# A fused attention and mixture-of-experts layer on one core: norm rows moved to GpSimd, ScalarE's copies and the giving out of tiles placed anew, VectorE's relus ahead of ScalarE's

## The chip, the cores and the metric

The kernel runs on one core of a Trainium2 chip. The metric is the time of the whole kernel on the device, in microseconds. The core has five engines that the text calls by the names of the profile: PE (TensorE, the matmuls), DVE (VectorE), ACT (ScalarE), POOL (GpSimd) and SP (SyncE, which here only starts transfers). Each works through its own instructions in order; semaphores hold an instruction until what it reads is there, or until the buffer that it writes is free.

## The reference, cut to what matters

x is 8 sequences (batches in what follows) of 512 tokens of 128 features, float32. A layer of attention with 16 heads of 8 features, causal, then a layer of 8 experts, of which each token takes the best two:

```python
def _layernorm(x, axis=-1, eps=1e-05):
    m = jnp.mean(x, axis=axis, keepdims=True)
    v = jnp.var(x, axis=axis, keepdims=True)
    return (x - m) / jnp.sqrt(v + eps)
...
    q = (x @ Wq).reshape(b, t, H, HD); k = ...; v = ...
    s = jnp.einsum('bqhd,bkhd->bhqk', q * scale, k)
    s = jnp.where(causal[None, None], s, -jnp.inf)
    p = jax.nn.softmax(s, axis=-1)
    o = jnp.einsum('bhqk,bkhd->bqhd', p, v).reshape(b, t, H * HD)
    return o @ Wo + bo
...
    logits = x_flat @ gate_w.T
    probs = jax.nn.softmax(logits / TEMPERATURE, axis=-1)
    topk_probs, topk_idx = jax.lax.top_k(probs, TOPK)
    hidden = jax.nn.relu(jnp.einsum('th,ehf->tef', x_flat, w1) + b1[None])
    all_out = jnp.einsum('tef,efh->teh', hidden, w2) + b2[None]
    gathered = jnp.take_along_axis(all_out, topk_idx[:, :, None], axis=1)
    y_flat = jnp.sum(gathered * topk_probs[:, :, None], axis=1)
...
    x = x + attention(_layernorm(x), ...)
    x = x + experts(_layernorm(x), ...)
```

## The kernel before

**Attention** goes batch by batch, and in a batch by four groups g of four heads. For a group the scores are computed twice. `shifts` computes them with queries in rows (tiles "s", PE lines L623 and L628) only for the maximum of each row (tile "pm", DVE, L642); the maxima (nm, L648) are split into two bf16 parts by GpSimd (nh, L358), transposed by PE (nmTp, L588), copied by ScalarE (nmT, L590) and written by GpSimd's own DMAs (L596) as two more rows into the operand q of the second product. `attend` then computes the scores transposed (tiles "st", L783 and L788), already less the row's maximum; ScalarE's exp turns a bank of them into "pt" (L793), and PE multiplies pt with the values "va" into "po" (L704). At a group's end po is copied (ob), transposed (oqp, L725), divided (L728, L730), and at a batch's end transposed once more (oTp, L748; copy oT, L750) and projected (pp, L756; added to x on DVE, L760).

s and st share a ring of four PSUM banks (`ps_sc`): an s bank is freed by a row maximum on DVE, an st bank by an exp on ACT. Everything else goes through a ring of three banks (`ps_mm`).

**Ahead of a batch's attention** `norms` (for b = 0 and 1 `project` itself) runs `layernorm`: statistics of four blocks of 128 tokens on DVE (bn_stats, bn_aggr, L369 and L370), two small operations on GpSimd (ve, rstd, L358), and four rows xn on DVE (L384, 128x128 each). `project` transposes xn (xnTp on PE, copy xnT on ACT, L397), computes q and k, splits them into three bf16 parts each (ACT, DVE and a subtraction on GpSimd, L478), packs them through DRAM, adds the bias bo to x on GpSimd (L553), and computes the values (pv on PE, L567; copy va on ACT, L571).

**Experts.** When a batch's attention is done, `route` normalises it with the same `layernorm` (xn_f), computes the logits (pl, L834), picks two experts, counts, gives each token a slot and scatters its row into DRAM by GpSimd's indirect DMAs (L1052). After batches 1, 3, 5, 6 and 7 `dispatch` (steps s = 0 to 4, DVE L962 to L1024) gives out tiles of 128 slots, 8, 16, 16, 23 and 15 of them, while other batches still run. A tile of an expert is four matmuls with the first weights (ph, L1287), a relu of each of the four columns c of blocks into hT, and four with the second weights (py, L1146). The relus go c = 0, 1, 2, 3: ACT takes two of them (three, once attention is over), DVE the rest (L1294 and L1296). They write one tile hT, and its writes are kept in the order in which they were traced.

**What orders the work.** Each of these parts is a Python generator that yields the time at which it wants to go on, in units of one batch; a loop always advances the one with the smallest time. For PE, ACT, DVE and SP the order in which instructions are traced in this way is the order on the engine. GpSimd's go through `G_ops`, which keeps program order as well. So a number such as `b - 1.84` is a place in the queue, and no wait by itself. In `route`, `soon(n)` moves its clock on by n steps; a step is 0.018 of a batch for b = 1, 3 and 5 and 0.025 for 0, 2 and 4, 0.012 for 6 and 7. The expert tiles have planned times of their own (`TILES_AT`), the first at 3.3.

```python
    TILES_AT = ((3.3, 0.24), (5.35, 0.12), (7.5, 0.055), (8.4, 0.03), (9.1, 0.03))
...
        while lanes:
            lane = min(lanes)
            try:
                lane[0] = max(lane[0], next(lane[2]))
```

Of the kernel before, what the change touches and what calls it, by code (L numbers as in the profile page):

```python
# [9 lines left out]
F32 = mybir.dt.float32  # L10
# [3 lines left out]
ALU = mybir.AluOpType  # L14
# [4 lines left out]
P = 128  # L19
# [7 lines left out]
def preln_attn_moe(ctx: ExitStack, tc: tile.TileContext, x, wq, wk, wv, wo, bo,  # L27
# [35 lines left out]
    nc = tc.nc  # L63
    V = nc.vector
    B, T, D = x.shape
    E, _, F = w1.shape
    H, HD = 16, 8
    NT = T // P
    G, HG = 4, 4
    NP = H // 2  # L70
    FC = F // P
# [33 lines left out]
    for k, b in ((0, 1), (0, 3), (0, 5), (0, 6), (1, 7)):  # L105
        n = GROUPS[k].index(b) + 1
# [14 lines left out]
    small = ctx.enter_context(tc.tile_pool(name="small", bufs=2))  # L121
# [18 lines left out]
    def load_x(b):  # L140
        t = const.tile([P, NT, D], F32, tag=f"x{b}", name=f"x_{b}")
        nc.sync.dma_start(out=t, in_=x[b].rearrange("(c p) d -> p c d", p=P))
        return t

    xt = {0: load_x(0)}
# [43 lines left out]
    for s in range(2):  # L189
# [3 lines left out]
        f = const.tile([P, P], BF16, tag=f"feature{s}", name=f"feature_{s}")  # L193
# [76 lines left out]
    def mm_tile(name):  # L270
        return ps_mm.tile([P, T], F32, tag="mm", name=name)
# [14 lines left out]
    for k in range(2):  # L286
        n = E * ROOM[k] + SPARE * P
# [77 lines left out]
    def layernorm(src, name, t, each):  # L365
        stats = small.tile([P, NT, 6], F32, tag="stats", name=f"stats_{name}")
        mv = small.tile([P, NT, 2], F32, tag="mv", name=f"mv_{name}")
        for c in range(NT):
            nc.vector.bn_stats(stats[:, c, :], src[:, c, :])  # L369
            nc.vector.bn_aggr(mv[:, c, :], stats[:, c, :])  # L370
            yield t[0] + each * (c + 1)
        rstd = small.tile([P, NT], F32, tag="rstd", name=f"rstd_{name}")
        ve = small.tile([P, NT], F32, tag="ve", name=f"ve_{name}")
        first = name in ("a0", "a1")
        on_pool = nc.gpsimd if first else G_ops
        on_pool.tensor_tensor(ve, mv[:, :, 1], eps, ALU.add)
        on_pool.tensor_tensor(rstd, ve, mhalf, ALU.pow)
        yield t[1]
        xn = work.tile(
            [P, NT, D if name[0] == "a" else XROW], F32, tag=f"xn{name[0]}", name=f"xn_{name}",  # L380
            bufs=1 if name[0] == "a" else XB,
        )
        for c in range(NT):
            nc.vector.tensor_scalar(  # L384
                xn[:, c, :D], src[:, c, :], mv[:, c, 0:1], rstd[:, c : c + 1],
                ALU.subtract, ALU.mult,
            )
            if c < NT - 1:
                yield t[1] + each * (c + 1)
        return xn  # L390

    def rows_T(xn, name):
        pt = mm_tile(f"xnTp_{name}")
        for c in range(NT):
            nc.tensor.transpose(pt[:, ts(c, P)], xn[:, c, :D], ident)
        xnT = work.tile([P, T], F32, tag=f"xnT{name[0]}", name=f"xnT_{name}", bufs=1)
        nc.scalar.copy(xnT, pt)  # L397
        return xnT


    normal = {}

    def norms():
        for b in range(2, B):
            yield b - 2.16
            normal[b] = yield from layernorm(xt[b], f"a{b}", (b - 2.16, b - 2.0), 0.025)


    packed, shifted, attended, added = set(), set(), set(), set()
# [2 lines left out]
    def project():  # L412
# [17 lines left out]
        for b in range(B):  # L430
            early = EARLY if b > 1 else 0.0
            if b < 2:
                yield b - 1.70
                xn = yield from layernorm(
                    xt[b], f"a{b}", (b - 1.70, b - (1.32 if b == 1 else 1.50)), 0.025
                )
            else:
                xn = normal.pop(b)
            if 0 < b < B - 2:
                xt[b + 2] = load_x(b + 2)  # L440
            yield b - (1.84 if b > 1 else 1.21 if b == 1 else 1.41)
            xnT = rows_T(xn, f"a{b}")
            late = 0.19 if b == 1 else 0.0
            yield b - (1.40 if early else 1.36) - early + late
# [2 lines left out]
            n = G if b == 0 else 2  # L447
# [112 lines left out]
                pack(0, 1)  # L560
                pack(1, 1)
            packed.add(b)
            yield b - 0.85
            assert b < 2 or b - 2 in added
            pv = mm_tile(f"pv_{b}")
            for c in range(NT):
# [245 lines left out]
    def route():  # L812
        for b in range(B):
# [6 lines left out]
            def soon(steps=1.0, least=0.0, step=step, least_of=float(b < B - 1)):  # L820
                now[0] += max(steps * step, least * least_of)
                return now[0]

            yield now[0]
            t = [soon(0), soon(7), soon(4 if b == B - 1 else 6)]
            xn2[b] = yield from layernorm(
                xt[b], f"f{b}", t, step / 2 if b == B - 1 else step
            )
# [38 lines left out]
            for k in range(2):  # L867
# [9 lines left out]
                f = pick[:, b, k, :].rearrange("p (c e) -> p c e", e=E)  # L877
# [64 lines left out]
            lanes.append([now[0], 100 + b, scatter(k, b, now[0])])  # L942
            for s, (_, after, _, _) in enumerate(STEPS):
                if after == b:
                    yield from dispatch(s, soon)


    def dispatch(s, soon):
# [130 lines left out]
    def when(s, i):  # L1079
        t0, pace = TILES_AT[s]  # L1080
        return t0 + pace * i

    def experts():
# [13 lines left out]
        def quad(s, i):  # L1097
            first = i - i % 4
            return first, min(4, STEPS[s][2] - first)

        def after(s, i):
            return when(s, quad(s, i)[0]) >= B

        def ahead(s, i):
            if not after(s, i):
                return 3

            late = [a for a in tiles if after(*a)].index((s, i))
            return min(WTS - 3, WTS // 2 - 2 + late)

        def behind(s, i):
            return 2 if after(s, i) else 1
# [27 lines left out]
        def second(s, i, hT):  # L1140
            first, m = quad(s, i)
            if i == first:
                yo[s, first] = work.tile([P, 4, D], F32, tag="yo", name=f"yo_{s}_{i}")
            py = mm_tile(f"py_{s}_{i}")[:, :D]
            for c in range(FC):
                nc.tensor.matmul(  # L1146
                    py, lhsT=hT[:, c, :], rhs=w2_sb[:, bass.ds(at[s, i] + c * E * D, D)],
                    start=(c == 0), stop=(c == FC - 1),
                )
            V.tensor_tensor(  # L1150
                yo[s, first][:, i - first, :], py, wt[s, i][:, F + FC :], ALU.add
            )
# [28 lines left out]
        def store(s, i):  # L1181
            k, b, _, last = STEPS[s]
            first, m = quad(s, i)
            ins = nc.gpsimd.indirect_dma_start(  # L1184
                out=ys[k],
                out_offset=bass.IndirectOffsetOnAxis(
                    ap=to[s, first][:, i - first : i - first + 1], axis=0
                ),
                in_=yo[s, first][:, i - first, :], in_offset=None,
            )  # L1190
            in_order(ins)
            for other in sent[k]:
                tc.declare_no_dep(
                    ins.ins, other, reason="every slot has its own row, or one nobody reads"
                )
            sent[k].append(ins.ins)
            if last and i == STEPS[s][2] - 1:
                tiled[k] = sent[k]
# [77 lines left out]
        for n, (s, i) in enumerate(tiles):  # L1276
            first, m = quad(s, i)
            yield when(s, i + 1)
            if after(s, i):
                ph = ps_sc.tile([P, T], F32, tag="sc", name=f"ph_{s}_{i}")  # L1280
                hT = work.tile([P, 2, T], F32, tag="pt", name=f"hT_{s}_{i}", bufs=6)
                hT = hT[:, 0, :].rearrange("p (c t) -> p c t", c=FC)
            else:
                ph = mm_tile(f"ph_{s}_{i}")
                hT = work.tile([P, FC, P], F32, tag="hT", name=f"hT_{s}_{i}")
            for c in range(FC):
                nc.tensor.matmul(  # L1287
                    ph[:, ts(c, P)], lhsT=wt[s, i][:, ts(c, P)],
                    rhs=turned[s, first][:, ts(i - first, P)], start=True, stop=True,
                )  # L1290
            for c in range(FC):
                bias = wt[s, i][:, F + c : F + c + 1]
                if c < (FC - 1 if after(s, i) else FC // 2):
                    nc.scalar.activation(hT[:, c, :], ph[:, ts(c, P)], AF.Relu, bias=bias)  # L1294
                else:
                    nc.vector.tensor_scalar(  # L1296
                        hT[:, c, :], ph[:, ts(c, P)], bias, 0.0, ALU.add, ALU.max
                    )
            yield when(s, i + 1.4)
            ready = late[: max(0, len(late) + 1 - behind(s, i))]  # L1300
            del late[: len(ready)]
            for part in ready:
                second(*part)
            yield when(s, i + 1.7)
            for part in ready:
                store(*part[:2])
            late.append((s, i, hT))
            fetch_to(n + 1 + ahead(s, i))
# [115 lines left out]
```

## Time and profile before

| what | value |
|---|---|
| median of 3 runs | 583.0 us (582.61 to 583.82) |
| the profiled execution's own time | 580.48 us |
| its span, first to last instruction | 578.8 us, granted PE clock 0.966 |
| PE busy | 506.7 us (88%) |
| DVE busy | 410.5 us (71%), 1272 instructions recorded |
| ACT busy | 307.3 us (53%) |
| POOL busy | 242.4 us (42%), 380 instructions recorded |
| first st of batches 1 to 7 | 88.3, 132.4, 178.4, 229.4, 280.3, 335.2, 389.8 us |
| row maxima (pm, L642) | 320, 680 ns each |
| exps (pt, L793) | 320, 599 ns each |

How to read the views. A row of instructions has start, duration, engine, line, operation, output and inputs by the program's names, and a count where several stand together; "[0.74 <-ACT pt L793]" behind it says that the engine was idle for 0.74 us before and that ScalarE's instruction of line 793 ended that. The waits of an engine are given as "who waited <- for whom: us in total, times, longest". The table by stretches has, for each engine, its busy time and the number of its instructions, then PEclk, the TensorE clock that was granted as a share of the full one, the share of DMA time, and GB/s. A busy PE can still be slow: where PEclk is 0.5, its matmuls take twice as long.

### The profile page before, as it was taken

How to read it: one execution, taken by the hardware profiler on the slowest of the kernel's cores; microseconds unless marked ns; L12 is line 12 of the kernel's file. 1: busy time of each engine (PE TensorE's matmuls, PEld its weight loads, DVE VectorE, ACT ScalarE, POOL GpSimd, SP SyncE). 2: the span in 40 equal slices, each digit the busy share in tenths (PEclk: the TensorE clock that was granted, in tenths of full speed). 3: DMA queues.
4: the chain of work that ended last, by engine and by line, in shares of the span. 5: the costliest groups of instructions: out<-in, count | busy, mean ns of one | idle time of the engine just before them, and what ended most of it. 6: DMA issues, size and time to landing. Idle time of an engine off the chain costs nothing. (4 is left out here: it accounts for less than half of the span.)

```text
span 578.8 us, 14044 instructions
## 1 busy us (share of the span) xinstructions
PE 506.7 (88%) x4762; PEld 373.9 (65%) x4762; DVE 410.5 (71%) x1272; ACT 307.3 (53%) x673; POOL 242.4 (42%) x380
## 2 busy tenths in 40 slices
PE   8868999988987989999899999998898889789980
PEld 6644556556544565665567777766576878689980
DVE  4987787887888779778978678787653445233694
ACT  3645666755754665575556555554564434245530
POOL 4032212405716423661753356345435524644442
PEclk9888899999998999999999999999999979989995
DMA  3728667288299572535526573222333686758783
GB/s 82 190 66 202 150 157 184 59 206 191 73 193 188 145 193 55 133 80 130 158 65 169 116 193 94 66 66 76 102 107 117 199 269 190 208 165 263 239 303 104
DMA packets 68761, 86.06 MB, mean 149 GB/s; under 512 B 11540, under 2 KB 50748, under 8 KB 66652
## 3 DMA queue, kind: packets, MB, share of 16 engines
q1 hardware_dynamic: 61508, 74.87, 50.0%
q0 software_dynamic: 6592, 9.65, 5.2%
q8 instruction: 39, 0.64, 0.5%
q10 hardware_dynamic: 592, 0.66, 0.5%
q14 instruction: 30, 0.25, 0.1%
HBM read 61.34 MB, written 26.16 MB: 151 GB/s over the span
## 5 line engine op out<-in xcount | busy, mean ns | idle before, releaser
L793 ACT ACTIVATE pt<-st 128x512 f32<-128x512 f32 x320 | 178.4, 599 | 109.0 <-PE st L783 49.3
L642 DVE TENSOR_REDUCE pm<-s 128x1 f32<-128x512 f32 (+2 forms) x320 | 205.5, 680 | 27.0 <-PE s L628 23.3
L1184 POOL DMA_INDIRECT ys<-yo,to x78 | 76.5, 980 | 99.1 <-ACT pt L793 32.4
L623 PE MATMUL s<-k,q 72*128 72x384 bf16 (+2 forms) x384 | 93.3, 278 | 15.8 <-ACT pt L793 9.9
L628 PE MATMUL s<-k,q 128*128 128x128 bf16 x512 | 94.1, 223 | 7.9 <-ACT pt L793 5.2
L783 PE MATMUL st<-q,k 128*128 128x128 bf16 x512 | 91.0, 220 | 10.2 <-DVE pm L642 5.5
L704 PE MATMUL po<-pt,va 128*18 128x512 f32 (+3 forms) x1024 | 91.6, 444 | 1.4 <-ACT pt L793 1.4
L788 PE MATMUL st<-q,k 74*128 74x256 bf16 (+2 forms) x384 | 91.9, 276 | 0.0
L1146 PE MATMUL py<-w_sb,hT 128*128 x624 | 87.4, 283 | 4.5 <-DVE have L962 2.2
L1146 PEld LDWEIGHTS py<-w_sb,hT 128*128 128x128 f32 x624 | 78.8, 197 | 7.8 <-issue 5.2
L1052 POOL DMA_INDIRECT xs<-xn_f,slot x64 | 64.0, 1000 | 30.9 <-ACT pt L793 15.6
L628 PEld LDWEIGHTS <-q 128*128 128x128 bf16 x512 | 50.9, 100 | 32.2 <-issue 29.2
L623 PEld LDWEIGHTS <-q 72*128 72x128 bf16 x384 | 37.6, 99 | 39.8 <-issue 32.2
L783 PEld LDWEIGHTS <-k 128*128 128x128 bf16 x512 | 50.9, 100 | 4.0
L788 PEld LDWEIGHTS <-k 74*128 74x128 bf16 x384 | 37.4, 98 | 22.7 <-issue 17.2
L596 POOL DMA_DIRECT2D q<-nmT x64 | 34.1, 536 | 39.5 <-ACT nmT L590 37.2
L358 POOL CAST nh<-nm 128x16 bf16<-128x16 f32 x28 | 5.6, 198 | 91.8 <-DVE nm L648 90.8
L1296 DVE TENSOR_SCALAR hT<-ph,wt 128x128 f32<-128x128 f32 x72 | 21.9, 346 | 28.8 <-ACT hT L1294 23.5
L704 PEld LDWEIGHTS po<-pt,va 128*18 128x18 f32 x1024 | 22.7, 96 | 30.1 <-issue 21.8
L1294 ACT ACTIVATE hT<-ph,wt 128x128 f32<-128x128 f32 x72 | 22.6, 364 | 35.7 <-issue 12.3
L1287 PE MATMUL ph<-xgT,wt 128*128 128x128 f32 x288 | 40.1, 282 | 0.7 <-issue 0.4
L1287 PEld LDWEIGHTS ph<-xgT,wt 128*128 128x128 f32 x288 | 35.0, 191 | 5.6 <-issue 2.7
(185 smaller groups left out, 697.6 us busy)
## 6 DMA issues: line engine op xcount, KB each, us to landing
wt<-wrows SPq DMA_DIRECT2D x36, 322.0 KB
k<-kparts SPq DMA_DIRECT2D x42, 192.0 KB
q<-wrows SPq DMA_DIRECT2D x24, 322.0 KB
k<-wrows SPq DMA_DIRECT2D x18, 322.0 KB
q<-qparts SPq DMA_DIRECT2D x30, 192.0 KB
q<-ys SPq DMA_DIRECT2D x15, 256.0 KB
k<-xs SPq DMA_DIRECT2D x42, 65.0 KB
qparts<-part SPq DMA_DIRECT2D x14, 192.0 KB
```

Of the source, the lines that this page charges most:

```text
L596: ins = nc.gpsimd.dma_start(out=q2_buf[b % 2][KS + l : KS + l + 1, HG * g : HG * g + HG], in_=nmT[16 * l : 16 * l + 16],)
L623: nc.tensor.matmul(ps[:, at : at + t * P], lhsT=q2[:KS, h, q], rhs=k2[:KS, h, : t * P], start=(at == 0), stop=True, skip_group_check=True,)
L628: nc.tensor.matmul(ps[:, at + t * P : at + (t + 1) * P], lhsT=q2[:, h, q], rhs=k2[:, h, q], start=(at + t == 0), stop=True, skip_group_che ...
L642: nc.vector.tensor_reduce(top, src, AX.X, ALU.max)
L704: nc.tensor.matmul(po[32 * h : 32 * h + 2 * VC, j * P :], lhsT=va[:, j, c0 : c0 + 2 * VC], rhs=at_cols(pts[pr], unit, u, at, W), start=(fi ...
L783: nc.tensor.matmul(ps[:, at : at + P], lhsT=k2[:, h, k], rhs=q2[:, h, k], start=(at == 0), stop=True, skip_group_check=True,)
L788: nc.tensor.matmul(ps[:, at + P : at + T - j * P], lhsT=k2[:KO, h, k], rhs=q2[:KO, h, (j + 1) * P :], start=False, stop=True, skip_group_c ...
L793: last_exp[0] = nc.scalar.activation(pt[:, v, :], ps, AF.Exp, scale=SCALE)
L1052: ins = nc.gpsimd.indirect_dma_start(out=xs[k], out_offset=bass.IndirectOffsetOnAxis(ap=slot[b][:, j * NT + i : j * NT + i + 1], axis=0), ...
L1146: nc.tensor.matmul(py, lhsT=hT[:, c, :], rhs=w2_sb[:, bass.ds(at[s, i] + c * E * D, D)], start=(c == 0), stop=(c == FC - 1),)
L1184: ins = nc.gpsimd.indirect_dma_start(out=ys[k], out_offset=bass.IndirectOffsetOnAxis(ap=to[s, first][:, i - first : i - first + 1], axis=0 ...
L1287: nc.tensor.matmul(ph[:, ts(c, P)], lhsT=wt[s, i][:, ts(c, P)], rhs=turned[s, first][:, ts(i - first, P)], start=True, stop=True,)
```

## The change

1. The statistics of batches 3 to 7 start at b - 2.5 on the planner's clock, where it was b - 2.16 (batch 2 stays).
2. The rows xn of batches 2 to 7 are made by GpSimd. It adds the negated mean and multiplies, so a small operation `mean` that negates four means is added for each batch. They take their place in GpSimd's program order.
3. In `project` the transposes of xn and the copy xnT of batches 2 to 7 come at b - 1.76 instead of b - 1.84. On ScalarE the copy stood right after the copies oT and va, and now stands behind the exp of a later block. pv and the copy to va of batches 2 to 7 come at b - 0.9 instead of b - 0.85: PE's pv moves from behind oTp to ahead of st_b_0_1 of the batch before.
4. In `route` the second half of the norm starts after 10 steps instead of 7 for batches 0 to 5, and `dispatch` after batches 1, 3 and 5 takes steps 1.8 times as long.
5. The four relus of a tile are traced from c = 3 down to c = 0, so those of DVE first; ACT's now follow DVE's in the writes of hT.

```diff
@@ layernorm
+        apart = name[0] == "a" and not first
+        if apart:
+            mean = small.tile([P, NT], F32, tag="mean", name=f"mean_{name}")
+            on_pool.tensor_scalar(mean, mv[:, :, 0], -1.0, 0.0, ALU.mult, ALU.add)
         for c in range(NT):
-            nc.vector.tensor_scalar(
-                xn[:, c, :D], src[:, c, :], mv[:, c, 0:1], rstd[:, c : c + 1],
-                ALU.subtract, ALU.mult,
-            )
+            if apart:
+                on_pool.tensor_scalar(
+                    xn[:, c, :D], src[:, c, :], mean[:, c : c + 1], rstd[:, c : c + 1],
+                    ALU.add, ALU.mult,
+                )
+            else:
+                nc.vector.tensor_scalar(
+                    xn[:, c, :D], src[:, c, :], mv[:, c, 0:1], rstd[:, c : c + 1],
+                    ALU.subtract, ALU.mult,
+                )
@@ norms
-            yield b - 2.16
-            normal[b] = yield from layernorm(xt[b], f"a{b}", (b - 2.16, b - 2.0), 0.025)
+            t = b - (2.16 if b == 2 else 2.5)
+            yield t
+            normal[b] = yield from layernorm(xt[b], f"a{b}", (t, t + 0.16), 0.025)
@@ project
-            yield b - (1.84 if b > 1 else 1.21 if b == 1 else 1.41)
+            yield b - (1.76 if b > 1 else 1.21 if b == 1 else 1.41)
...
-            yield b - 0.85
+            yield b - (0.9 if b > 1 else 0.85)
@@ route
-            t = [soon(0), soon(7), soon(4 if b == B - 1 else 6)]
+            t = [soon(0), soon(7 if b >= B - 2 else 10), soon(4 if b == B - 1 else 6)]
...
-                    yield from dispatch(s, soon)
+                    wide_steps = 1.0 if b >= B - 2 else 1.8
+                    yield from dispatch(s, lambda n=1.0: soon(n * wide_steps))
@@ experts
-            for c in range(FC):
+            for c in reversed(range(FC)):
                 bias = wt[s, i][:, F + c : F + c + 1]
                 if c < (FC - 1 if after(s, i) else FC // 2):
                     nc.scalar.activation(hT[:, c, :], ph[:, ts(c, P)], AF.Relu, bias=bias)
```

## The prediction

> **What bounds the kernel now.** I read the page first (PE busy 88% of 578.8 us, DVE 71%, ACT 53%, POOL 42%), so TensorE's own work sets the time wherever it is not made to wait. Then a table by stretches of time, one row per batch or stage:
>
> ```profile
> core 0: us, PE busy (x) PEld busy (x) DVE busy (x) ACT busy (x) POOL busy (x), PEclk, DMA share, GB/s
> ...
> 178.00:229.00 51.00, 45.37 (x442) 29.55 (x442) 41.43 (x117) 30.31 (x61) 19.34 (x32) 0.97 0.58 136
> ...
> 335.00:390.00 55.00, 52.56 (x543) 39.15 (x543) 43.12 (x131) 30.62 (x67) 26.52 (x42) 1.00 0.38 105
> ...
> 503.00:579.00 76.00, 54.37 (x459) 53.00 (x457) 39.29 (x156) 27.50 (x88) 32.60 (x34) 0.89 0.69 216
> ```
>
> While attention runs (to about 440 us) PE has 2.4 us (335 to 390) to 5.6 us (178 to 229) of idle time in a batch of 51 to 55, with DVE second at 41 to 43. After 445 there is no attention; the order there changes only in the relus. So the change can win attention's idle time and little else. What ends those waits of PE, from 80 to 440 us (columns: us in total, times, longest):
>
> ```profile
> PE s L623 <- ACT pt L793: 9.4, 19, 1.5
> PE s L628 <- ACT pt L793: 5.2, 10, 0.6
> PE st L783 <- DVE pm L642: 5.1, 12, 2.2
> PE st L783 <- ACT pt L793: 2.3, 5, 0.7
> PE s L628 <- DVE pm L642: 2.2, 4, 0.8
> ```
>
> These five make 24.2 us of about 27: PE waits for one of four PSUM banks, which an exp (ACT, 16.9 us) or a row maximum (DVE, 7.3 us) frees. Last, VectorE's and ScalarE's order around the worst stretch:
>
> ```profile
> 178.87 0.22 DVE L992 TENSOR_TENSOR past<-ends,number 128x64 f32<-128x64 f32 x1
> 179.12 0.22 DVE L996 TENSOR_REDUCE own<-past 128x8 f32<-128x64 f32 x1
> ...
> 181.10 0.34 DVE L384 TENSOR_SCALAR xn_a<-x,mv_a,rstd_a 128x128 f32<-128x128 f32 x1
> 181.35 0.22 DVE L1010 SCALAR_TENSOR_TENSOR slotno<-jump,begins,place_no 128x8 f32<-128x8 f32 x1
> ...
> 183.01 0.60 DVE L384 TENSOR_SCALAR xn_a<-x,mv_a,rstd_a 128x128 f32<-128x128 f32 x2
> 183.53 1.28 DVE L642 TENSOR_REDUCE pm<-s 128x1 f32<-128x512 f32 x2
> ```
>
> The giving out of tiles (dispatch, s=0) and the norm rows of a later batch sit between the row maxima, and PE stands 0.49 (178.41), 0.22 (179.01), 0.26 (182.01) and 0.74 us (183.14): 1.7 us. Right after, from 184.0 to 187.4, the granted clock is 0.51 and four transposes for oqp take 1.12 us instead of 0.66: some 1.7 us more.
>
> **The change, part by part.** Sums are against the profiled execution: span 578.8, 580.5 with the 1.7 around it. The median shown is 583.0, that is 2.5 above; I add 2.5 at the end.
>
> *Rows by GpSimd.* 24 rows of 128x128 (L384) leave VectorE for batches 2 to 7: back to back they start 0.26 to 0.31 us apart (the pair at 183.01 takes 0.60), so 24 x 0.30 = 7.2 us, 1.2 us a batch, of 41. That is paid to PE only where DVE frees the bank last (7.3 of 24.2 us). The earlier statistics (8 small instructions a batch, about 17 us sooner for batches 3 to 7) only move. I take -2 us; bounds 0 (all hidden) and -5 (all named waits but the 2.2 us one, which has another cause, below). GpSimd's price for a row is not in the trace. Nearest rows: 128x4 TENSOR_SCALAR 0.239 us (L358), 128x512 two-input add 1.281 (L553) and subtract 1.165 (L478). A quarter of 1.165-0.2 over a fixed 0.2 gives 0.45 as an estimate; four rows and the new negation are 2.0 us a batch, 5.3 at the upper end. They stand before the add of bo (1.28 us) and the row DMAs of the group (L596) in GpSimd's fixed order. For batch 1 those DMAs start at 80.03 and the first st that reads them is at 88.33: 8.3 us of room for 2.0 to 5.3 more, beside the landing. Cover in time, cost 0; if it is gone, each batch would pay up to 5.3-(8.3-landing), some 1 to 2 us.
>
> The Trainium skill, GPSIMD Engine Reference, section 4.1 speaks against this part: elementwise work belongs on VectorE, GpSimd being about twice as slow with two inputs and near line rate with one. The trace agrees for two inputs (1.165 us against 0.693 for the same subtract on DVE). By that rule a row would be about 0.35 to 0.7 us, 1.4 to 2.8 a batch, and as it stays inside the 8.3 us the sum is the same.
>
> *ScalarE's copies.* xnT_a (0.58 us) comes after oT and va (0.59, 0.60) at 188.3 to 190.2 with an exp behind; now it comes after the second exp of a later block, its four transposes filling a wait of PE: 0.52 us at 100.31, 0.5 at 144 and the like in 193 and 242, 0.23 at 295. Four transposes are 0.44 us: 4 x 0.44 = -1.8. pv (0.89 us of PE) and the copy to va move ahead of an st where PE waits 0.26 to 0.3: -0.3 x 6 at most, I take -0.8. If the waits only slip behind the filler, both are 0; if the copy holds an exp up by its whole 0.6 us, +3. Two x loads change place by one on SP, long before use: 0.
>
> *Giving out of tiles.* Steps 1.8 times as long after batches 1, 3 and 5, the norm of the second half later by three steps (3.5 us). Available: 1.7+1.7 (s=0), 1.35 (0.39+0.22+0.74 us near 281), 2.1 (0.62 at 389.6 and 1.49 at 394.6): 6.9 us. The instructions stay, and what they displace slips somewhere else, so I take 4.0; bounds 0 and -6.9. Later rows for scatters and gathers are covered: the first tile's relu is at 207.32, the dispatch ends at 183.2.
>
> The clock first as the rows show it: 0.51 for 3.4 us, though the largest single gap before was 0.74 us. TensorE: Matmul & The Clock Gate, Part 1, has the clock halved after an idle window of about 3.4 us, free-running. The step's length agrees; the idle before it does not, as PE was busy 1.24 of the 2.0 us before 184. By the rule nothing would be halved there and smaller gaps would win only 5.2 of the 6.9 us.
>
> *Relus.* Before, DVE's wait for ACT's, because both write one tile in order:
>
> ```profile
> DVE hT L1296 <- ACT hT L1294: 49.7, 38, 5.7
> ```
>
> 34.9 of this is after 440, where PE never waits for DVE in turn and two tiles lie between: 0 there. Now ACT's wait for DVE's. In the 24 tiles of s=0 and 1, inside attention, DVE can go 9.4 us sooner in sum (its 9.2 us of waits from 200 to 420 go), but ACT can start later only when DVE is through its row maxima (1.28 a pair) and its own relus (0.61 a pair). Example: ACT's pair at 267.68 would wait for DVE's from 269.31 on, 2.3 us, with two exps queued behind it; at 207.32 only 0.65. Laid tile by tile, ACT's delays sum to about 28 us. The bank an exp frees is wanted a median 1.35 us later, so most of it is absorbed: after subtracting that slack at most 17 us are left for PE; at best nothing and the 6 us where DVE was last. Bounds -6 and +17; I take +3.6, as ACT waits for PE 28.1+16.9 us between 200 and 420 and catches up soon.
>
> Untouched: PE's 2.2 us at 411, where DVE waits 3.0 for rstd_f behind GpSimd's indirect DMAs, and the 4.9 us gap at 503.5.
>
> Sum: -2.0 -1.8 -0.8 -4.0 +3.6 = -5.0; 580.5 -5.0 +2.5 = **578.0 us**.
>
> **Rivals.** (1) *ACT's exps queue behind VectorE's relus.* Place: the 24 tiles between about 207 and 417 us. Half of the 28 us (13.6) reaches PE: 583.0 -8.6 +13.6 = 588.0, slower. For it: two exps stand right behind each pair, and DVE is the fuller engine (41 against 30 us). Against it: ACT's 45 us of waits for PE. It decides from 8.6/24 = 0.36 us of PE time a tile on.
> (2) *All of it pays, relus cost nothing.* -3.0 -1.8 -0.8 -5.4 = -11.0: 572.0.
> (3) *It does not do what it says:* row maxima still come 1.28 us a pair, the spread instructions hit other row maxima, PE's waits only change place: 583.0.
> (4) *Rows late:* GpSimd at its upper price, or slowed by DVE, pushes the row DMAs past the first st, 2 us a batch over six, against -5: 583 -5 +12 = 590.
>
> **Chances.** Forecast 0.47 (its own range 574 to 581.5), (1) 0.25, (2) 0.15, (3) 0.09, (4) 0.04. About 0.2% (1.2 us) is what a measurement of this kernel can tell from no change. Faster: 0.47+0.15 = 0.62; same 0.09; slower 0.25+0.04 = 0.29. The range to hold 8 in 10 runs from 569 (all of (2) and half of the relus' 6 us) to 590 (the value of (1), 588, and of (4)); most of the chance, but not all of it, is on the faster side.
>
> **What would show it.** Rows right: POOL rows at about 0.45 us, DVE busy 1.2 us less a batch, no wait of PE for q's rows. Copies: the 0.5 us waits at 100, 144, 193, 242 gone. Spread: no clock of 0.5 near 184, the waits near 281 and 390 below half. Relus: no DVE wait for ACT's hT; a wait of ACT for DVE's hT below some 10 us between 200 and 420 speaks for the forecast, over 20 with PE's waits for pt above 17 us for (1). Wrong altogether if batches shorten where no dispatch is, or the stretch after 445 moves by over 2 us.

## The result, and the profile after

The changed kernel is slower: 604.84 us in the median of 4 runs (602.73 to 612.53) against 583.41 us in the median of 4 (582.61 to 584.33), a ratio of 1.0354 with a 95% interval of 1.0325 to 1.0384. The forecast of 578.0 was wrong, and the time lies outside its range of 569 to 590. The medians count every run, the ratios only runs in the faster of the two states that runs of one kernel show, and the profiled execution of after is in the slower one (612.53 us, span 610.8). So its single places are read here, and sizes are taken from other runs too, above all from e5_after, the same kernel once more (606.24 us in its profile).

The same table by stretches, for batches 3 and 6 and the tail, which now start at 187, 360 and 534 us:

```profile
core 0: us, PE busy (x) PEld busy (x) DVE busy (x) ACT busy (x) POOL busy (x), PEclk, DMA share, GB/s
187.00:240.00 53.00, 46.98 (x442) 29.91 (x442) 40.96 (x120) 29.92 (x61) 22.75 (x38) 0.97 0.52 127
360.00:415.00 55.00, 52.23 (x542) 39.33 (x541) 41.61 (x123) 29.75 (x67) 24.93 (x43) 1.00 0.39 104
534.00:611.00 77.00, 57.08 (x491) 55.16 (x490) 40.19 (x158) 28.55 (x94) 34.22 (x36) 0.93 0.71 218
```

Batch 6 and the tail are nearly as they were (PE 52.2 of 55 against 52.6; from the last exp to the end 126.7 us against 128.8). So the loss is not spread: compared exp by exp with the profile of before, the changed kernel falls behind by about 7 us between 44 and 80, 6 us between 257 and 269, 5 between 295 and 307 and 6 between 405 and 419 (times of before), with smaller steps between. In the profile of e5_after these four steps are 2, 6, 3 and 6 us. PE's waits, from 87 to 470 us:

```profile
PE st L794 <- DVE pm L653: 11.3, 10, 3.4
PE s L634 <- ACT pt L804: 5.7, 11, 1.0
PE st L794 <- ACT pt L804: 3.8, 5, 1.7
PE s L634 <- DVE pm L653: 3.2, 5, 1.5
PE xgTp L1258 <- DMA xg<-xs: 2.3, 4, 1.1
PE s L639 <- DVE pm L653: 1.6, 4, 0.8
PE pl L845 <- ACT xnT_f L407: 1.1, 1, 1.1
```

Each row has what PE waited to start, who ended it, the us in total, the times and the longest. In the rows listed, waits for exps went from 16.9 to 9.5 us and waits for row maxima from some 7.6 to 16.1, though VectorE has fewer instructions. Two kinds are new: xgTp for gathered rows, and pl for a copy of ScalarE. What changed ahead of them shows in ScalarE's own waits, over the whole trace of after:

```profile
ACT hT L1307 <- DVE hT L1309: 52.4, 30, 5.0
```

It is the mirror image of VectorE's 49.7 us in 38 waits before. One of them, first the tile's matmuls, then ScalarE and VectorE from 312 us:

```profile
311.52 1.11 PE L1299 MATMUL ph<-xgT,wt 128*128 128x128 f32 x8
```

```profile
314.86 0.62 ACT L1307 ACTIVATE hT<-ph,wt 128x128 f32<-128x128 f32 x2 [5.01 <-DVE hT L1309]
315.37 0.60 ACT L804 ACTIVATE pt<-st 128x512 f32<-128x512 f32 x1
315.85 0.59 ACT L407 COPY xnT_a<-xnTp_a 128x512 f32<-128x512 f32 x1
```

```profile
312.46 1.28 DVE L653 TENSOR_REDUCE pm<-s 128x1 f32<-128x512 f32 x2
313.66 0.16 DVE L1030 TENSOR_SCALAR taken<-first 128x8 f32<-128x8 f32 x1
313.85 0.17 DVE L1031 SCALAR_TENSOR_TENSOR taken<-taken,free 128x8 f32<-128x8 f32 x1
314.05 0.17 DVE L1033 TENSOR_TENSOR given<-given,taken 128x8 f32<-128x8 f32 x1
314.17 0.61 DVE L1309 TENSOR_SCALAR hT<-ph,wt 128x128 f32<-128x128 f32 x2
314.69 0.28 DVE L369 BATCH_NORM_STATS2 stats_f<-x 128x6 f32<-128x128 f32 x1
```

The tile's ph is complete at 312.63. VectorE first does a pair of row maxima and three instructions of the dispatch and then its own pair of relus, so ScalarE's relus start at 314.86, 2.2 us after ph was there, and two copies and the exps of two st blocks queue behind them. The 5.0 us in the row are ScalarE's whole idle time; up to 312.63 it would have stood for ph in any case. The same tile before:

```profile
293.28 1.11 PE L1287 MATMUL ph<-xgT,wt 128*128 128x128 f32 x8
294.42 0.62 ACT L1294 ACTIVATE hT<-ph,wt 128x128 f32<-128x128 f32 x2 [2.62 <-PE s L628]
```

There ScalarE starts as soon as ph is complete (294.39). In after, PE then waits 1.65 us at 315.82, and from 317.2 it runs at half clock for 3.4 us.

GpSimd's rows, from the table of groups:

```profile
L358 POOL TENSOR_SCALAR xn_a<-x,mean_a,rstd_a 128x128 f32<-128x128 f32 x24 | 10.4, 447 | 0.7
```

### The profile page after: what moved, and what is told of

Its sections match the earlier page's. It is cut to its first block, busy times and chain, and to the rows that moved or that the text cites. A ratio compares the mean times of both kernels' runs of the same rounds, so it can differ in the third digit from the quotient of the medians.

```text
span 610.8 us, 14073 instructions
## 1 busy us (share of the span) xinstructions
PE 527.2 (86%) x4762; PEld 383.5 (63%) x4762; DVE 409.8 (67%) x1248; ACT 305.1 (50%) x673; POOL 253.8 (42%) x410
## 4 chain that ended last, share of the span: by engine, by line
PE 51%; DVE 21%; issue 8%; ACT 8%; DMA 6%; POOL 3%; SPq 3%; DVEq 0%; ACTq 0%; POOLq 0%; another core or an unknown queue 0%
PE po L715 10%; DVE pm L653 10%; PE ph L1299 7%; PE py L1158 7%; PE st L799 5%; PE s L634 4%; ACT pt L804 4%; PE st L794 4%; PE s L639 3%; ACT hT L1307 2%; PE pq L479 2%; DVE hT L1309 2%; DMA q<-nmT 2%; PE pl L845 1%; DMA q<-ys 1%
## 5 line engine op out<-in xcount | busy, mean ns | idle before, releaser
L653 DVE TENSOR_REDUCE pm<-s 128x1 f32<-128x512 f32 (+2 forms) x320 | 206.2, 681 | 49.7 <-PE s L639 46.5
L794 PE MATMUL st<-q,k 128*128 128x128 bf16 x512 | 93.2, 225 | 21.6 <-DVE pm L653 11.9
L634 PE MATMUL s<-k,q 72*128 72x384 bf16 (+2 forms) x384 | 96.1, 285 | 15.4 <-ACT pt L804 6.2
L715 PE MATMUL po<-pt,va 128*18 128x512 f32 (+3 forms) x1024 | 98.4, 467 | 1.6 <-ACT pt L804 1.6
L639 PE MATMUL s<-k,q 128*128 128x128 bf16 x512 | 95.6, 226 | 3.5 <-DVE pm L653 1.6
L799 PE MATMUL st<-q,k 74*128 74x256 bf16 (+2 forms) x384 | 95.8, 285 | 0.0
L799 PEld LDWEIGHTS <-k 74*128 74x128 bf16 x384 | 38.4, 100 | 31.1 <-issue 25.2
L794 PEld LDWEIGHTS <-k 128*128 128x128 bf16 x512 | 52.6, 103 | 8.0 <-issue 3.4
L715 PEld LDWEIGHTS po<-pt,va 128*18 128x18 f32 x1024 | 24.8, 99 | 32.1 <-issue 21.8
L1307 ACT ACTIVATE hT<-ph,q 128x128 f32<-128x128 f32 x72 | 21.2, 366 | 32.2 <-DVE hT L1309 19.7
```

The costliest lines, as they stand in the source:

```text
L634: nc.tensor.matmul(ps[:, at : at + t * P], lhsT=q2[:KS, h, q], rhs=k2[:KS, h, : t * P], start=(at == 0), stop=True, skip_group_check=True,)
L639: nc.tensor.matmul(ps[:, at + t * P : at + (t + 1) * P], lhsT=q2[:, h, q], rhs=k2[:, h, q], start=(at + t == 0), stop=True, skip_group_che ...
L653: nc.vector.tensor_reduce(top, src, AX.X, ALU.max)
L715: nc.tensor.matmul(po[32 * h : 32 * h + 2 * VC, j * P :], lhsT=va[:, j, c0 : c0 + 2 * VC], rhs=at_cols(pts[pr], unit, u, at, W), start=(fi ...
L794: nc.tensor.matmul(ps[:, at : at + P], lhsT=k2[:, h, k], rhs=q2[:, h, k], start=(at == 0), stop=True, skip_group_check=True,)
L799: nc.tensor.matmul(ps[:, at + P : at + T - j * P], lhsT=k2[:KO, h, k], rhs=q2[:KO, h, (j + 1) * P :], start=False, stop=True, skip_group_c ...
```

## The experiments

Three theories. **A**: ScalarE's relus wait for VectorE's and hold up the exps. **B**: GpSimd's rows delay the row DMAs. **C**: the spread makes scatters, and what is queued behind them, late. The times of before differ by chip, so each run goes with the run of before on its own chip and the ratio counts. First, one part at a time.

**e1_relu**, before with the reversal alone:

```diff
-            for c in range(FC):
+            for c in reversed(range(FC)):
                 bias = wt[s, i][:, F + c : F + c + 1]
```

> The kernel before with the reversed relus and nothing else. Theory A (ScalarE's relus wait for VectorE's, the exps behind them hold PSUM banks, and PE then also loses its full clock): in the changed kernel the places with such tiles, from 204 to 229, 257 to 280 and 295 to 308 on the time scale of before, fell behind by 4.5, 7.7 and 6.2 us, 18.4 in sum, so about 600 us here (594 to 604), with a wait of ACT for DVE's hT and more stretches at half clock after 200 us. The rivals (B, rows on GpSimd; C, later scatters) put the loss elsewhere: 581 to 587 here.

Measured: 595.82 (before 585.55), 1.0178 (1.0077 to 1.0280). About 10 us: at the lower end of A's span, far over its rivals'. ScalarE's waits for VectorE's hT from 180 to 445 us are 23.1 us in 11, and PE's waits of st for row maxima rise from 3.6 to 8.8.

**e2_after_no_relu**, the changed kernel with the old order put back:

```diff
-            for c in reversed(range(FC)):
+            for c in range(FC):
```

> The changed kernel with the relus in their old order, all else changed. Theory A: 604.8 - 18.4 = 586 us (582 to 591). If B and C make the loss, 600 or more. If the parts only hurt together, neither this nor the relus alone shows 18 us.

Measured: 586.23, 1.0051 (0.9993 to 1.0108). A's number. All the other parts together change nothing that this measurement can clearly tell from before.

**e3_norms**, before with earlier statistics and GpSimd's rows (the parts layernorm and norms of the change's diff):

> The kernel before with the statistics sooner and the rows of batches 2 to 7 on GpSimd. Theory B (in batch 0 the row DMAs of the second group start 1.0 us later, behind the rows, and land 5.3 us later, behind the packing transfers; PE waits 2.9 us and loses its clock): 7 us later by the first st of batch 1 (88.3 before), then some gain from VectorE's 7 us less: 586 to 591. Rival: rows cost nothing and VectorE's relief pays, 579 to 583.

Measured: 585.84, 1.0060 (1.0013 to 1.0108). By the ratio a small loss, by the medians (585.55 before) none; where I had forecast a gain there is none. It is at the lower edge of what B expects. The row DMAs of batch 0's second group landed late, at 56.1 us, and PE waited 0.6 for them, not 2.9.

**e4_spread**, before with the later second norm and the wider dispatch (the part route of the diff):

> The kernel before with the second norm later and dispatch spread, nothing else. My forecast's term: -4 us, 579. Theory C (the scatters that GpSimd issues come later, so that rstd_f waits longer behind them at about 411 us of before, where the changed kernel fell behind by 5.8 us and by 3.7 more to 477): 585 to 593.

Measured: 587.21, 1.0050 (0.9997 to 1.0103). Not my -4, and at the lower end of C. The trace shows a gain of 1.6 us over the dispatch of s=0 and a loss of 3.1 from 195 to 217, where there is a new wait, of xgTp for gathered rows: 1.0 us in three.

Why does ScalarE wait at all? My prediction said that the writes of one tile hT are kept in order. The second reason possible is that both engines read one PSUM bank, ph. **e5_after** is the changed kernel, to go with the next three on one chip:

> The changed kernel once more, beside the following ones on one chip: 1.03 times the kernel before, as measured, so 600 to 607 us where before is 583 to 586; ACT's waits for DVE's hT near the 24 us of its first profile.

Measured: 604.07 (before 583.99), 1.0332 (1.0248 to 1.0417).

**e6_after_split_ht**, two tiles of SBUF:

```diff
-                hT = work.tile([P, FC, P], F32, tag="hT", name=f"hT_{s}_{i}")
+                halves = [
+                    work.tile([P, FC // 2, P], F32, tag=f"hT{n}", name=f"hT{n}_{s}_{i}")
+                    for n in range(2)
+                ]
+                hT = [halves[c // (FC // 2)][:, c % (FC // 2), :] for c in range(FC)]
```

> The changed kernel with hT of the tiles inside attention in two tiles of SBUF, one that ScalarE writes and one that VectorE writes. Theory A1 (ACT waits because the writes of one tile hT are kept in order, as the prediction had it): the waits of ACT for DVE's hT go, and with them some 17 us: 586 to 591. Theory A2 (ACT waits because both read the same PSUM bank ph): nothing changes, 600 to 607 and 24 us of waits.

Measured: 602.55, 1.0287 (1.0196 to 1.0378). A1, the prediction's reason, falls: the time and the waits stay. ScalarE's waits from 180 to 445 us in this kernel:

```profile
ACT hT L1312 <- DVE hT L1314: 21.9, 9, 5.0
```

**e7_after_two_banks**, ph in two of the three banks:

```diff
-                ph = mm_tile(f"ph_{s}_{i}")
+                ph = [mm_tile(f"ph_{s}_{i}_{n}")[:, : T // 2] for n in range(2)]
+                ph = [ph[c // (FC // 2)][:, ts(c % (FC // 2), P)] for c in range(FC)]
```

> The changed kernel with ph of the tiles inside attention in two PSUM banks of the ring of three, one for ScalarE's two columns and one for VectorE's. Theory A2: no wait of ACT for DVE's hT any more but where the ring itself makes it; about 588 us (584 to 593), as without the reversal. Rival: the ring of three is short now and PE waits for its banks, 595 to 610. Theory A1: 600 to 607, the waits stay.

Measured: 583.76, 0.9984 (0.9939 to 1.0030). The whole loss is gone, 20.3 us against e5_after, with the relus still traced in the reversed order. PE's waits from 180 to 445 us, first in e5_after, then in e7_after_two_banks:

```profile
PE st L794 <- DVE pm L653: 9.4, 6, 3.3
PE st L794 <- ACT pt L804: 4.0, 5, 1.9
PE s L634 <- DVE pm L653: 3.2, 5, 1.5
PE s L634 <- ACT pt L804: 3.1, 5, 1.0
```

```profile
PE s L634 <- ACT pt L804: 5.4, 9, 1.0
PE st L794 <- DVE pm L653: 2.6, 3, 2.1
PE xgTp L1258 <- DMA xg<-xs: 1.9, 6, 0.5
PE st L794 <- ACT pt L804: 1.0, 2, 0.7
```

The long waits of st, for row maxima and for exps, are what the reversal brought. ScalarE no longer waits for VectorE's hT in this stretch. The edit gives ph two tiles as well as two banks, so these runs don't say which of the two, the shared tile or the shared bank, makes one engine wait for the other.

**e8_two_banks**, the same edit in the kernel before:

> The kernel before with ph in two banks in the same way, relus in their old order. VectorE's 14.8 us of waits for ScalarE's hT between 180 and 445 go. If these cost something: 577 to 582. If they lay in idle time: 582 to 586. If the ring of three is short: over 587.

Measured: 585.23, 1.0047 (1.0003 to 1.0090). VectorE's 14.8 us of waits for ScalarE are gone from its list and the time is not better: they lay in idle time. It isn't that the less busy engine waited: VectorE was busy 41.4 of the 51 us of batch 3, ScalarE 30.3. In the old order ScalarE took its relus within 0.3 us of ph and itself being ready, so what is queued behind them was not held up by VectorE.

Then the small parts, on a chip where before takes 565.74. **e9_norms_from_3**, as e3_norms but for batch 2's rows:

```diff
-        apart = name[0] == "a" and not first
+        apart = name[0] == "a" and name not in ("a0", "a1", "a2")
```

> The kernel before with the statistics sooner and the rows on GpSimd for batches 3 to 7 only; batch 2's rows, which GpSimd made ahead of the second group's row DMAs in batch 0, stay on VectorE. Theory B (the late landing of those DMAs costs 1 to 6 us in the runs so far): 1 to 3 us under the kernel with all six batches moved, so 581 to 584, the same as before or a little better; the last row of the second group lands by about 53.5 us and PE does not wait for q's rows. Rival (rows on GpSimd cost elsewhere, or nothing): as with all six, 1.006 times before, 586 to 588.

Measured: 563.26, 0.9980 (0.9929 to 1.0031). The row DMAs landed at 52.8 us and PE had no wait for them. Against e3_norms (1.0060, on another chip) the estimates lie as B has it, but their intervals overlap.

**e10_project**, the two moved copies alone (the part project of the diff):

> The kernel before with the moved copies alone (xnT_a and its transposes at b - 1.76, pv and va at b - 0.9). My forecast's terms: -2.6 us. The changed kernel with two banks (583.8) shows no such gain beside the others, so I expect 583 to 585, the waits of 0.5 us at 100 and 144 gone and others in their place; rival, the terms as forecast: 580 to 582.

Measured: 564.84, 1.0022 (0.9993 to 1.0052). No gain; the forecast's -2.6 us would be 0.9955.

**e11_relu_spread**, the edits of e1_relu and e4_spread together:

> The kernel before with the reversed relus and the later second norm and dispatch. The reversal alone cost 1.8%, in the changed kernel 3.0%. If the spread instructions are what makes VectorE late for its relus (more of them stand between row maxima, and the indirect DMAs at about 425 us then wait for ScalarE's held exps): 600 to 606. If the difference lies in the rows or the copies: 593 to 598.

Measured: 591.41, 1.0492 (1.0430 to 1.0554). More than the changed kernel's loss and than either expectation, but on another chip than e1_relu.

**e12_dispatch_only**, the wider dispatch without the later second norm:

```diff
-                    yield from dispatch(s, soon)
+                    wide_steps = 1.0 if b >= B - 2 else 1.8
+                    yield from dispatch(s, lambda n=1.0: soon(n * wide_steps))
```

> The kernel before with dispatch 1.8 times as wide, the second norm where it was. With both, PE lost its 2.5 us gain at 178 to 194 again from 195 to 217, where xgTp waits for gathered rows (1.0 us in three waits) and the expert tiles meet other work. If the later second norm (scatters late, so gathers late) makes that: no waits of xgTp for xs there, 581 to 583. If the later row numbers of the dispatch itself do: the waits stay, 585 to 588.

Measured: 566.66, 1.0029 (0.9981 to 1.0077). The waits of xgTp for xs are gone from 190 to 217 us, so the later second norm makes them. No gain in time that could be told.

What was left: how 8 us more of waits become 20 us. I measured in the profiles the stretch from the first exp of batch 3 to the last exp, the idle time of PE that is recorded in it, and the time at a granted clock of one half:

| kernel | stretch, us | PE idle | at half clock |
|---|---|---|---|
| before | 271.1 | 21.1 | 3.4 |
| e5_after | 294.6 | 28.6 | 30.7 |
| e1_relu | 285.1 | 25.6 | 20.5 |
| e7_after_two_banks | 271.9 | 18.6 | 3.4 |

For e5_after, 7.5 us more idle and half of 27.3 more at half clock, 13.7, make 21.2 of the 23.5 lost; for e1_relu 4.5 and 8.6 make 13.1 of 14.0. That is bookkeeping over one profile of each kernel, and shows no cause. To test the clock as a cause (theory D), **e13_after_filled** puts PE to work in the waits:

```diff
+            if (s, i) in ((0, 0), (0, 3), (0, 4), (0, 5), (0, 7), (1, 7), (1, 15)):
+                keep_warm(10, f"{s}_{i}")
```

> The changed kernel with ten idle matmuls (128x256 bf16, some 1.07 us, into a free bank) behind ph of the seven tiles after which PE waited 1.5 us or more; seven times 1.07 = 7.5 us more of PE's work, laid into waits that VectorE's order sets. Theory D (a stretch of 3.41 us with PE busy under about 65% is followed by one at half clock, and half of the loss is that): of 30.7 us at half clock in batches 3 to 7 half go, the time falls by 4 to 8 us below the changed kernel on the same chip. Rival (the slow stretches are no cause, the waits alone are): the same time as the changed kernel or up to 7 us more.

**e14_relu_again** to **e16_after_again** ran on the same chip as it:

> The kernel before with the reversed relus alone, once more beside the next two on one chip. If the reversal costs more only together with the spread dispatch: 1.018 times before, as before. If the larger cost of 1.049 was the other chip's: 1.03 or more where the next run shows as much.

> The reversed relus and the spread, once more beside the others on one chip. Theory E (the spread puts more of VectorE's small instructions ahead of its relus, so that PE's waits fall closer together and more stretches run at half clock): at least 10 us above the relus alone. Rival (the chip made the difference): within 5 us of it.

> The changed kernel on the same chip, to be compared with the three others: 1.033 times before. If VectorE's relief by the rows on GpSimd works, it lies 5 us or more below the relus with the spread.

| kernel | median, us | ratio to before (585.22) |
|---|---|---|
| e13_after_filled | 607.64 | 1.0385 (1.0311 to 1.0459) |
| e14_relu_again | 596.86 | 1.0186 (1.0127 to 1.0246) |
| e15_relu_spread_again | 602.20 | 1.0302 (1.0233 to 1.0371) |
| e16_after_again | 604.58 | 1.0291 (1.0213 to 1.0370) |

In the profiles the filled kernel had 13.7 us at half clock in batches 3 to 7 against 17.1 for e16_after_again, and it was no faster: D's gain did not come. The seven fillings kept PE busy for 8.8 us, which cost time where no wait hid them, and each took a bank of the ring of three, so this run can't say that the clock costs nothing, only that these fillings did not pay. The same kernel had 30.7 us at half clock in e5_after and 17.1 here, so the clock's share of the loss is not a fixed one. The reversal costs 1.8% alone on two chips. With the spread it is 5.3 us more, between E's 10 and its rival's 5, so theory E is neither shown nor refuted; of the 4.9% on the other chip this chip shows 3.0. Nor do the rows on GpSimd and the moved copies show a relief (602.20 without them, 604.58 with them).

## Why the prediction was wrong, point by point

**The relus** (+3.6, bounds -6 to +17) is the step that failed: the term was some five times too small. It measured 17.8 us in the changed kernel (e5_after less e2_after_no_relu, on one chip) and 20.3 by e7_after_two_banks, 10 to 12 alone. The mechanism was rival (1), with its direction, place and two exps queued behind a pair; I gave it 0.25 and 588. Of the two signs named for it one came, ScalarE's waits for VectorE's hT over 20 us (22.8 in e5_after between 180 and 445 us). The other did not: PE's waits for exps fell, and those for row maxima rose.

The delay of ScalarE that I laid out (28 us over 24 tiles) was of the right size. In e5_after its relus in these tiles start 0.7 to 2.8 us after both ph and ScalarE were ready, 31.1 us in sum; before, it was at most 0.3 us, 1.7 in sum. "The bank an exp frees is wanted a median 1.35 us later, so most of it is absorbed" is half right: PE's idle time in batches 3 to 7 rose by 7.5 us (table above), a quarter of the delay, but twice the 3.6 that I took. What the term left out is the clock: there were 27.3 us more at half clock, 13.7 us of loss by the bookkeeping, and the term has nothing for it, nor has its bound of 17, although I had counted 1.7 us for the clock at the dispatch of s=0. That this half of the loss comes from the clock is argued, not shown by a run.

"ACT catches up soon" was no ground either: as I read it, when ScalarE stands, PE stops for want of banks and VectorE then lacks blocks of s, so ScalarE's free time between 200 and 420 us is not at hand where it is needed. VectorE's waits for s ahead of its row maxima rose from 8.2 us to 24.2 in e5_after (180 to 445 us), which fits.

The reason given for the wait was wrong too, here and in the description of the kernel: not the writes of one tile hT, but ph, the one tile in one PSUM bank that both engines read (e6_after_split_ht and e7_after_two_banks).

**The tail** (no cost of the relus after attention) held: 20 of ScalarE's 30 waits for VectorE's hT in the profile of after, 28.2 of the 52.4 us, come after the last exp, and PE does not fall further behind there.

**The rows** were priced rightly at 0.45 us: 0.447 measured. "Cover in time, cost 0" was worked out for batch 1 (8.3 us of room) and not for batch 0, where the packing transfers of batch 1 run. There the row DMAs of the second group were issued 1.0 us later (48.28 against 47.26) and their last packet ended at 57.50 instead of 52.16; PE waited:

```profile
PE st L794 <- DMA q<-nmT: 2.9, 1, 2.9
```

In the eight profiles with batch 2's rows on GpSimd these DMAs ended at 55.3 to 57.5 us, and in three of them PE waited 2.0 us or more for them: after, e6_after_split_ht and e7_after_two_banks (2.8), whose time is that of before. In e2_after_no_relu and e3_norms the wait was at most 0.6. VectorE's relief, 7.2 us and -2 in the sum, hardly came: its recorded busy time fell from 410.5 us to 409.8 in after, to 408.4 in e3_norms and to 407.5 in e2_after_no_relu, although the 24 rows had left; what took up the rest was not followed. The ratio of e9_norms_from_3, 0.998 (0.993 to 1.003), can't tell -2 us from nothing.

**The copies** (-2.6) measured nothing (e10_project 1.0022). In the profile of after the waits of s on line 639 for exps from 100 to 190 us fell from before's 1.9 to 0.5, as said, those on line 634 from 3.2 to 2.4, while the waits for row maxima rose from 2.2 to 2.8: the places were filled, the time not won.

**The spread** (-4.0) measured +0.3 to +0.5%, not clear of zero. It was predicted that the cover "the first tile's relu is at 207.32, the dispatch ends at 183.2" holds; but the gathers wait for scatters that the later second norm pushes back, and xgTp waits for the gathers. Of the 1.7 us of PE's waits ahead of 184, the trace puts 1.0 (182.01 and 183.14) down to exps and not to the row maxima that the dispatch stood between. The half-clock step near 184 is gone in e4_spread, as said, but there is one from 204.9 to 208.3 in its place.

So of the -8.6 us of gains nothing is to be seen (e7_after_two_banks 0.998, e2_after_no_relu 1.005). Rival (3), PE's waits change place, is what the profiles show for the copies and the spread; rival (1) holds for the relus. The waits that a profile lists were not a store from which a sum could be drawn; that this is because VectorE, 78 to 81% busy in attention, does the row maxima one behind the other, is argued.

## What to carry to other kernels

Where two engines read one buffer and are made to wait for each other, look at which of them gets to it first and at what is queued behind the one that waits. Here the order that let ScalarE, which was there at once, go first cost nothing. The opposite order made it wait for VectorE's queue, 0.7 to 2.8 us a tile, and cost 1.8% alone and 3% in the changed kernel, although ScalarE was the less busy engine; two tiles in two banks removed the wait. When a change adds waits of the matmul engine, look for the time at half clock that may follow, beside the standing. A wait named in a profile is worth its time only if the engine that ends it is late for that reason alone.

## What the runs showed of the hardware

A half clock follows a stretch of low use; the stretch need not be idle. The clock changes in steps of 3.41 us. I laid all 18 profiles out in such steps between 60 and 440 us and took, for each step at full clock, the share of it in which the matmul records have PE busy. The step after it ran at half clock in 25 of 26 cases where PE was busy less than 50%, in 46 of 74 from 50 to 65%, in 10 of 70 from 65 to 75%, and in 3 of 1716 above 75%. Two gaps of 0.7 us in one step leave it 59% busy, in the band with 46 of 74. The Trainium skill, TensorE: Matmul & The Clock Gate, Part 1, has the step's length right; its table of the clock's two states puts the half clock after at least one idle window, and here a step with 35 to 50% of idle time was enough in 46 of 74 cases.

GpSimd's small row DMAs (4 KB each) took longer when they were issued behind SP's transfers. In the ten profiles in which the second group's row DMAs of batch 0 were issued 0.7 to 0.9 us ahead of SP's first packing transfer of k (192 KB), the last packet came 4.9 to 7.1 us after the issue (4.9 in before, issued at 47.26). In the eight with batch 2's rows on GpSimd they were issued 0.1 to 0.3 us behind that transfer, and it came after 6.5 to 9.2 us (9.2 in after, issued at 48.28). e9_norms_from_3, which leaves batch 2's rows on VectorE and moves those of 3 to 7, is among the ten, with 5.25 us. That SP's transfers are what holds them up is argued from this.
